# A two-layer graph network: where the edge lists of the nodes are built, and when the list writes are issued

## The chip, the cores and the metric

The kernel runs on one core of a Trainium2 chip. The core has five engines with instruction queues of their own: PE (TensorE: matmuls), DVE (VectorE), ACT (ScalarE), POOL (GpSimd) and SP (SyncE, which here only issues transfers). The metric is the device time of one launch in microseconds (us); lower is better. Each engine executes its instructions in the order in which they were laid down, and waits at one of them until what it needs is there. Indirect transfers (gather: rows of a table by a list of indices; scatter: rows to a table by a list of indices) are issued by POOL, plain transfers by SP or ACT.

## What is computed

There are 1250 nodes with 768 features and 20000 directed edges, sorted by destination, with one of 34 types each.

```
h  = relu(layernorm(x))
h  = gatv2(h, 8 heads, W1s, W1d, attn1) ; h = layernorm(h + relu(layernorm(x)))
h  = gatv2(h, 1 head, Wos, Wod, attno)  ; x = x + layernorm(h)
gatv2: fs = x Ws + bs ; fd = x Wd + bd ; per edge e = leaky_relu(fs[src] + fd[dst]) . attn
       softmax of e over the edges of a destination ; out = elu(sum alpha * fs[src])
h  = relu(layernorm(x))
mean[r, n] = mean of h[src] over the edges of type r into node n
h1 = sum over r of mean[r] W_rel[r] + h W_root + b
out = x + gcn(h1)        (symmetric normalisation by degrees + 1, one dense layer)
```

## The kernel before

Nodes are handled in ten tiles of 128, ordered by falling degree, so that a tile needs as many edge slots as its first node has edges: `CAPS = (33, 22, 20, 18, 17, 16, 15, 14, 13, 11)`, 179 slots in all. One slot of one tile is called a row here: for each of 128 nodes, one source node.

**Front** (`fast_front`). It loads x and edges, normalises x (`norm_scale`, L782 to L788) and transposes it (`to_columns`). Four things follow.

- The table: `sources(j)` (L807) makes tile j of `f_fs_d`, the projected sources with eight extra columns, by 26 matmuls on PE, two copies on ACT and a store on SP. `head_sums` (L795) makes the extra columns of the weights on DVE. Its PSUM tiles share the tag "ag" (two buffers, in the order written) with the ranking's.
- The ranking: L752 to L772 count for each node how many rows of 32 edges end before it, ten gathers (L777, `got`) fetch the row in which its edges begin, and `first` (L829) is the number of its first edge; the degree is the difference of neighbours, for which one matmul (L832) fetches the next partition's value. Keys of degree and number are spread to all partitions by matmuls (L859, L860) and compared by ten instructions (L865); the sum is the rank. Ten scatters (L880) write number, first edge and degree by rank into `rank_d`, and L901 reads it back in ranked order.
- The edges, after the ranking and in ranked order: ten gathers (L912) fetch 64 packed edges per node from `win_d`, and L916 to L931 shift them to the node's first edge, into `f.ell` and the source numbers `f.srci`.
- `pairs()` (L937 to L1069): for each edge the place in a list by type, with two sets of matmuls (L970 to L979) that count over partitions, and much DVE work. Its result goes to DRAM (`place_d`, L1069).

What sets the order: the program is laid down engine by engine by a planner with a cost model of its own. Of the instructions that it holds ready for an engine it takes the one written first; `tc.issue_after(i)` adds that an instruction comes behind `i` on its engine. In the front the table's tiles 0 and 1 are put around L832, keys behind tile 1, and tile 2 behind keys, by hand.

**Attention 1** (`attention`, called at L1444). For each row one gather (L1148) fetches 128 source rows into one of 24 buffers (`ring`), and three DVE instructions make z (L1208, L1213) and its sums (L1214). Rows are taken in chunks of at most 20; after a chunk comes its softmax, then ACT scales the rows and PE adds them (L1258 to L1268). After a tile's last chunk `finish1` (L1420) normalises, makes the rows of the second layer's tables and scatters them (`fs2`, by `scatter` at L1152). `negated1` fetches a tile's own rows (`h`) and makes the destination term `nfd` with 24 matmuls on PE.

**The lists.** Beside attention 1, 179 scatters (L1152, `r_pair_d`), one for each row, write the edges' records into `pair_d` by their places. They have no work of their own before them but `pairs()`, and a fill: `prepare_lists` (L1349) writes padding records into all of `pair_d` and zeros behind two later tables, makes these in SBUF and loads the places back (L1375). `list_edges(row, n)` (L1385) adds `n` to a count and issues as many writes behind the gather `row`. It is called with 0.9 after each row but the first 20, and with 60 after the very last, which issues all that are left (36).

Attention 2 and the 34 types follow, and a last dense layer. They are not touched.

Of the kernel before, what the change touches and what calls it, by code (L numbers as in the profile page):

```python
# [18 lines left out]
P = 128  # L19
# [607 lines left out]
def fast_front(ctx, tc, f, x, src, dst, edge_type, W1s, b1s, W1d, b1d, attn1, attno, W_rel):  # L627
# [34 lines left out]
    rank_d = dram.tile([NP, 4], I32, name="f_rank_d")  # L662
# [9 lines left out]
    f.ell = keepp.tile([P, NT, S0], I32, name="f_ell")  # L672
# [4 lines left out]
    f.place_d = dram.tile([P, NT * S0], I32, name="f_place_d")  # L677
    f.w1d = const.tile([P, KC, D], F32, name="f_w1d")

    with ExitStack() as front:  # L680
# [110 lines left out]

        quarter = SLOPE / (1.0 - SLOPE)
# [29 lines left out]
        last = sources(0)  # L822
# [8 lines left out]
        with tc.issue_after(last.ins):  # L831
            last = nc.tensor.matmul(sh_ps[:, 0:1], shift, first[:, 0:1], start=True, stop=True)  # L832
        with tc.issue_after(last.ins):
            last = sources(1)
# [3 lines left out]


# [14 lines left out]
        with tc.issue_after(last.ins):  # L854
            for g in range(2):
                wide = ps_m.tile([P, 2, 512], F32, name="wide", tag="ag").rearrange("p a b -> p (a b)")
                for lo, hi in ((0, 512), (512, N // 2)):
                    at = slice(g * (N // 2) + lo, g * (N // 2) + hi)
                    nc.tensor.matmul(wide[:, lo:hi], ones16[:EP], flat2[:, at], start=True, stop=False)  # L859
                    last = nc.tensor.matmul(wide[:, lo:hi], big16[:EP], flat[:, at], start=False, stop=True)  # L860
                nc.scalar.copy(keys[:, g * (N // 2):(g + 1) * (N // 2)], wide[:, :N // 2])
# [7 lines left out]
        rec = prep.tile([P, NT, 4], I32, name="rec")  # L869
        nc.vector.memset(rec, 0)  # L870
        nc.vector.tensor_copy(rec[:, :, 0], node)
        nc.vector.tensor_copy(rec[:, :, 1], first[:, :NT])
        nc.vector.tensor_copy(rec[:, :, 2], deg)

        past = prep.tile([NP - N, 4], I32, name="past")
# [10 lines left out]
        with tc.issue_after(last_keys.ins):  # L886
            sources(2)


        packed = prep.tile([EP, EC], I32, name="packed")  # L890
        nc.vector.scalar_tensor_tensor(packed, ev[:, 2, :], 2048.0, ev[:, 0, :], op0=ALU.mult, op1=ALU.add)
        zrow = prep.tile([1, RW], I32, name="zrow")
        nc.vector.memset(zrow, 0)
        pk = packed.rearrange("p (r c) -> p r c", c=RW)
        nc.scalar.dma_start(win_d[1:NR + 1, :RW].rearrange("(p r) c -> p r c", p=EP), pk)
        nc.scalar.dma_start(win_d[0:NR, RW:].rearrange("(p r) c -> p r c", p=EP), pk)
        nc.scalar.dma_start(win_d[NR:NR + 1, RW:], zrow)


        rk = prep.tile([P, NT, 4], I32, name="rk")  # L900
# [3 lines left out]
        nc.vector.tensor_copy(f.degf, rk[:, :, 2])  # L904
        arow = prep.tile([P, NT], I32, name="arow")
        nc.vector.tensor_scalar(arow, rk[:, :, 1], 5, None, op0=ALU.arith_shift_right)
        nc.vector.tensor_scalar(arow, arow, float(NR - 1), 1.0, op0=ALU.min, op1=ALU.add)
        offs = prep.tile([P, NT], I32, name="offs")
        nc.vector.tensor_scalar(offs, rk[:, :, 1], RW - 1, None, op0=ALU.bitwise_and)
        win = prep.tile([P, NT, WIN], I32, name="win")  # L910
        for k in range(NT):
            nc.gpsimd.indirect_dma_start(  # L912
                out=win[:, k, :], out_offset=None, in_=win_d[:, :],
                in_offset=bass.IndirectOffsetOnAxis(ap=arow[:, k:k + 1], axis=0))
        wf = prep.tile([P, NT, WIN], F32, name="wf")
        nc.vector.tensor_copy(wf, win)  # L916
        bits = prep.tile([P, 5, NT], F32, name="bits")
        for i in range(5):
            bi = prep.tile([P, NT], I32, name="bi", tag="bi", bufs=2)
            nc.vector.tensor_scalar(bi, offs, i, 1, op0=ALU.arith_shift_right, op1=ALU.bitwise_and)  # L920
            nc.vector.tensor_copy(bits[:, i, :], bi)
        for i in (4, 3, 2, 1, 0):
            b = 1 << i
            L = S0 + b - 1
            df = prep.tile([P, NT, S0 + 15], F32, name="df", tag="df")
            nc.vector.tensor_sub(df[:, :, :L], wf[:, :, b:b + L], wf[:, :, :L])
            nc.vector.tensor_tensor(df[:, :, :L], df[:, :, :L],
                                    bits[:, i, :, None].to_broadcast([P, NT, L]), op=ALU.mult)
            nc.vector.tensor_add(wf[:, :, :L], wf[:, :, :L], df[:, :, :L])
        nc.vector.tensor_copy(f.ell, wf[:, :, :S0])  # L930
        nc.vector.tensor_scalar(f.srci, f.ell, 2047, None, op0=ALU.bitwise_and)  # L931
# [5 lines left out]
        def pairs():  # L937
# [13 lines left out]
            typ = pp.tile([P, NT, S0], I32, name="typ")  # L951
            nc.vector.tensor_scalar(typ, f.ell, 11, None, op0=ALU.arith_shift_right)
            tv = pp.tile([P, NT, S0], F16, name="tv")
            nc.vector.scalar_tensor_tensor(tv, pad, 100.0, typ, op0=ALU.mult, op1=ALU.add)
# [101 lines left out]
            pl_i = pp.tile([P, NT, S0], I32, name="pl_i")  # L1056
# [11 lines left out]
            nc.vector.scalar_tensor_tensor(pl_i, pad, float(P * COLS), pl, op0=ALU.mult, op1=ALU.add)  # L1068
            nc.sync.dma_start(f.place_d[:, :], pl_i.rearrange("p k s -> p (k s)"))  # L1069

        for j in range(3, NT):
            sources(j)
# [53 lines left out]
def fast_rest(ctx, tc, f, x, src, dst, edge_type, W1s, b1s, W1d, b1d, attn1, ln1_w, ln1_b,  # L1126
# [9 lines left out]
    h2_d = dram.tile([NP + P, D], F32, name="r_h2_d")  # L1136
    ZERO = NP + (PT + 1) * P
    h1_d = dram.tile([ZERO + 1, D], F32, name="r_h1_d")
    pair_d = dram.tile([P * f.COLS, 3], I32, name="r_pair_d")
# [11 lines left out]
    def scatter(table, rows, idx, group, **kw):  # L1151
        s = nc.gpsimd.indirect_dma_start(  # L1152
            out=table, out_offset=bass.IndirectOffsetOnAxis(ap=idx, axis=0), in_=rows, in_offset=None, **kw)
        tc.declare_no_dep(s.ins, group=group, reason="every node's row is written once")
        tc.add_to_no_dep_group(group, s.ins)

# [15 lines left out]
    def attention(H, table, negated, attn_e, first, loads, finish, rate, rest):  # L1172
# [21 lines left out]
        def front(c, i):  # L1194
# [5 lines left out]
            if s >= CHUNK or t.k:  # L1200
                list_edges(row, rate)
            if t.k == NT - 1 and s == t.S - 1:
                list_edges(row, rest)
            if t.lg is None:
# [144 lines left out]
    def prepare_lists():  # L1349
# [3 lines left out]
        with tc.tile_pool(name="r_fill", bufs=1, side="right") as fp:  # L1353
            lane = rp.tile([P, 1], F32, name="lane")
            nc.gpsimd.iota(lane, pattern=[[0, 1]], base=NP, channel_multiplier=1,
                           allow_small_or_imprecise_dtypes=True)
            fill = fp.tile([P, COLS, 3], I32, name="fill")
            nc.vector.memset(fill[:, :, 2], 0)
            ones_c = fp.tile([P, COLS], F32, name="ones_c")
            nc.vector.memset(ones_c, 1.0)  # L1360
# [10 lines left out]
            for t in range(PT + 1):  # L1371
                nc.sync.dma_start(h1_d[NP + t * P:NP + (t + 1) * P, :], zero)
# [362 lines left out]
```

## Time and profile before

| | us |
|---|---|
| median of nine runs | 2773.75 |
| lowest and highest | 2768.9, 2782.42 |
| the profiled execution | 2778.29 |
| its span in the profile | 2776.4 |
| busy: PE, DVE, POOL, ACT | 2359.7, 1566.6, 1525.5, 854.1 |
| first row gathered, first z | 153.9, 184.3 |
| first and last list write | 221.4, 853.6 |
| first gather of attention 2 | 899.7 |

Times in the profile count from the start of the span. "Busy" is the sum of an engine's instructions; issuing, waiting and branching are not in it. In the timeline a line gives the start, the duration, the engine, the line of the program and the operation, output<-inputs, and in brackets how long the engine was idle before it and who ended that. A window's line gives, after its length, the busy time of PE, of PE's weight loads, of DVE, ACT and POOL with their instructions in brackets, then the granted PE clock, the busy share of the DMA engines and GB/s.

### The profile page before, as it was taken

How to read it: one execution, taken by the hardware profiler on the slowest of the kernel's cores; microseconds unless marked ns; L12 is line 12 of the kernel's file. 1: busy time of each engine (PE TensorE's matmuls, PEld its weight loads, DVE VectorE, ACT ScalarE, POOL GpSimd, SP SyncE). 2: the span in 40 equal slices, each digit the busy share in tenths (PEclk: the TensorE clock that was granted, in tenths of full speed). 3: DMA queues.
4: the chain of work that ended last, by engine and by line, in shares of the span. 5: the costliest groups of instructions: out<-in, count | busy, mean ns of one | idle time of the engine just before them, and what ended most of it. 6: DMA issues, size and time to landing. Idle time of an engine off the chain costs nothing. (4 is left out here: it accounts for less than half of the span.)

```text
span 2776.4 us, 24188 instructions
## 1 busy us (share of the span) xinstructions
PE 2359.7 (85%) x7759; PEld 1369.0 (49%) x7759; DVE 1566.6 (56%) x2361; ACT 854.1 (31%) x2308; POOL 1525.5 (55%) x1113
## 2 busy tenths in 40 slices
PE   6953685788888386888789999999999999999688
PEld 3521242444444143544456666666666666666254
DVE  5599979998975999999363222222222322210262
ACT  3004765767762132333311211221212211212010
POOL 1343877777873776776275554444444554431471
PEclk9976897999989788999889999999999999999899
DMA  6155443444431866675387777777777777766783
GB/s 212 44 165 181 128 131 97 128 132 134 137 93 38 278 203 202 208 216 178 123 265 189 191 190 192 185 189 197 192 193 199 187 188 189 182 162 152 213 266 121
DMA packets 136548, 476.85 MB, mean 172 GB/s; under 512 B 26185, under 2 KB 28514, under 8 KB 136413
## 3 DMA queue, kind: packets, MB, share of 16 engines
q0 software_dynamic: 83712, 334.44, 46.6%
q1 hardware_dynamic: 48043, 134.21, 13.6%
q10 hardware_dynamic: 4658, 6.57, 0.7%
q8 instruction: 64, 1.05, 0.2%
q14 instruction: 71, 0.58, 0.1%
HBM read 385.91 MB, written 89.33 MB: 171 GB/s over the span
## 5 line engine op out<-in xcount | busy, mean ns | idle before, releaser
L1116 PE MATMUL ps<-wrel,mT 128*128 128x384 f32 x3336 | 1099.6, 486 | 1.0 <-DMA wrel<-in_L_gnn_W_rel_dram 1.0
L1116 PEld LDWEIGHTS ps<-wrel,mT 128*128 128x128 f32 x3336 | 623.4, 190 | 407.2 <-issue 1.3
L1148 POOL DMA_INDIRECT g<-r_h_d,lists x241 | 340.4, 1413 | 525.6 <-DVE g L1580 286.2
L1268 PE MATMUL ag<-fs,identf 128*128 128x384 f32 x716 | 290.7, 540 | 165.4 <-ACT fs L1266 155.7
L1580 DVE TENSOR_TENSOR g<-g,g 128x768 f32<-128x768 f32 x68 | 64.6, 949 | 614.7 <-DMA g<-r_h_d,lists 420.5
L1208 DVE TENSOR_TENSOR z<-fs,nfd 128x776 f32<-128x776 f32 (+1 forms) x358 | 348.1, 990 | 45.2 <-DMA fs<-f_fs_d,rec 24.5
L1266 ACT ACTIVATE fs<-fs,lg 128x96 f32<-128x96 f32 x1376 | 370.7, 364 | 2.2 <-issue 1.7
L1258 PE MATMUL ag<-fs,dg 128*128 128x384 f32 x716 | 249.2, 509 | 81.1 <-ACT dg L1256 42.8
L1148 POOL DMA_INDIRECT fs<-f_fs_d,rec x179 | 251.1, 1403 | 101.1 <-issue 47.6
L1268 PEld LDWEIGHTS ag<-fs,identf 128*128 128x128 f32 x716 | 135.8, 205 | 307.6 <-ACT fs L1266 237.8
L1603 POOL DMA_INDIRECT r_h_d<-y,lists x139 | 224.1, 1612 | 109.8 <-ACT y L1602 52.1
L1148 POOL DMA_INDIRECT fs<-r_fs_d,rec x179 | 238.9, 1334 | 81.8 <-issue 31.4
L1152 POOL DMA_INDIRECT r_pair_d<-rec,place x179 | 234.8, 1311 | 85.1 <-issue 47.3
L1258 PEld LDWEIGHTS ag<-fs,dg 128*128 128x128 f32 x716 | 140.6, 199 | 186.1 <-ACT dg L1256 88.0
L1602 ACT ACTIVATE y<-ps,lists 128x768 f32<-128x768 f32 x71 | 64.1, 902 | 479.5 <-PE ps L1116 479.5
L1602 ACT ACTIVATE y<-ps,rcnt 128x768 f32<-128x768 f32 x68 | 61.4, 902 | 455.3 <-PE ps L1116 455.3
L1210 DVE SCALAR_TENSOR_TENSOR z<-z,attn_o 128x769 f32<-128x769 f32 x179 | 176.9, 1007 | 0.6 <-ACT dg L1256 0.5
L1665 DVE TENSOR_TENSOR acc<-acc,nb 128x768 f32<-128x768 f32 x69 | 66.2, 959 | 187.1 <-DMA nb<-r_h_d,srcz 183.3
L1213 DVE TENSOR_TENSOR z<-z,attn 128x776 f32<-128x776 f32 x179 | 168.6, 957 | 0.1
L1214 DVE TENSOR_REDUCE lg<-z 128x8 f32<-128x776 f32 x179 | 168.3, 952 | 0.1
L1513 DVE SCALAR_TENSOR_TENSOR arow<-node,from_f,arow 128x1250 f16<-128x1250 f16 x110 | 166.2, 1511 | 1.7
L1106 ACT COPY mT<-pt 128x384 f32<-128x384 f32 x278 | 119.2, 486 | 26.1 <-PE pt L1104 26.1
(283 smaller groups left out, 2298.6 us busy)
## 6 DMA issues: line engine op xcount, KB each, us to landing
wrel<-in_L_gnn_W_rel_dram SPq DMA_DIRECT2D x37, 2304.0 KB
g<-r_h_d,lists POOLq DMA_INDIRECT x241
r_nfd_d<-fd SPq DMA_DIRECT2D x10, 384.0 KB
nfd<-r_nfd_d SPq DMA_DIRECT2D x10, 384.0 KB
r_x_d<-xb SPq DMA_DIRECT2D x10, 384.0 KB
x1r<-r_x_d SPq DMA_DIRECT2D x10, 384.0 KB
f_fs_d<-o_s SPq DMA_DIRECT2D x9, 388.0 KB
x<-in_x_dram SPq DMA_DIRECT2D x9, 384.0 KB
```

What stands on the lines that cost most here:

```text
L1116: last = nc.tensor.matmul(ps[:n, half, :f.HW], hT[:, k, j * P:j * P + n], w[:, k, cols], start=(k == 0), stop=(k == f.KC - 1 and not bias))
L1148: return nc.gpsimd.indirect_dma_start(out=to, out_offset=None, in_=table, in_offset=bass.IndirectOffsetOnAxis(ap=idx, axis=0))
L1152: s = nc.gpsimd.indirect_dma_start(out=table, out_offset=bass.IndirectOffsetOnAxis(ap=idx, axis=0), in_=rows, in_offset=None, **kw)
L1208: nc.vector.tensor_tensor(z, fs, t.nfd, op=ALU.max)
L1210: nc.vector.scalar_tensor_tensor(z[:, 0, :], z[:, 0, :], 1.0, attn_e[:, 0, :], op0=ALU.mult, op1=ALU.mult, accum_out=t.lg[:, s, :])
L1213: nc.vector.tensor_mul(z, z, attn_e)
L1214: nc.vector.tensor_reduce(t.lg[:, s, :], z, axis=AX.X, op=ALU.add)
L1258: nc.tensor.matmul(c.ps[:, half, :HW], dg, fs[:, 0, half * HW:(half + 1) * HW], start=begin, stop=end)
L1266: nc.scalar.activation(fs[:, h, :HD], fs[:, h, :HD], AF.Copy, scale=t.lg[:, s, h:h + 1])
L1268: nc.tensor.matmul(c.ps[:, half, :HW].rearrange("p (h d) -> p h d", d=HD), f.identf, fs[:, half * H // 2:(half + 1) * H // 2, :HD], start= ...
L1513: nc.vector.scalar_tensor_tensor(a, node16, from_f[:, k, s:s + 1], a, op0=ALU.is_equal, op1=ALU.add)
L1603: s = nc.gpsimd.indirect_dma_start(out=h1_d[:, :], out_offset=bass.IndirectOffsetOnAxis(ap=j.node, axis=0), in_=y, in_offset=None, compute ...
```

## The change

1. **Edges in node order.** The edges are fetched and shifted for the nodes in their own order, from `first`, not from the ranked order. `arow`, `offs` and the ten gathers now stand right behind `first`, the shift behind the compares. The ranked record grows from 4 numbers to 2 + 33: number, degree and the 33 edges. Behind the read-back two instructions split source and type (`f.typ`); `f.ell` is gone.
2. **Order on PE.** L832 and the keys come without table tiles before them; tile 0 is behind the keys' last matmul, and tiles 1 to 9 are written after it.
3. **The fill in the front.** The padding records, the zeros and their eight stores are made behind the transposes of x, in the front's own pool.
4. **Places stay in SBUF.** `f.place` is written by DVE; the way over `place_d` is gone.
5. **List writes.** 30 behind row 23 of tile 0 (the last that has a free buffer), 0.85 behind each later row, 4 behind the last row, 7 behind the `fs2` scatter of tile 7, and what is left (7) behind that of tile 8.

```diff
-    rank_d = dram.tile([NP, 4], I32, name="f_rank_d")
+    rank_d = dram.tile([NP, 2 + S0], I32, name="f_rank_d")
...
-    f.place_d = dram.tile([P, NT * S0], I32, name="f_place_d")
+    f.place = keepp.tile([P, NT, S0], I32, name="place")
...
+        lane = keepp.tile([P, 1], F32, name="lane")
+        nc.gpsimd.iota(lane, pattern=[[0, 1]], base=NP, channel_multiplier=1,
+                       allow_small_or_imprecise_dtypes=True)
+        fill = prep.tile([P, COLS, 3], I32, name="fill")
...
+        nc.sync.dma_start(f.pair_d.rearrange("(p c) f -> p c f", p=P), fill)
+        zero = prep.tile([P, D], F32, name="zero")
+        nc.vector.memset(zero, 0.0)
+        nc.sync.dma_start(f.h2_d[NP:, :], zero)
+        for t in range(PT + 1):
+            nc.sync.dma_start(f.h1_d[NP + t * P:NP + (t + 1) * P, :], zero)
+        nc.sync.dma_start(f.h1_d[f.ZERO:, :], zero[:1])
...
-        last = sources(0)
...
-        with tc.issue_after(last.ins):
-            last = nc.tensor.matmul(sh_ps[:, 0:1], shift, first[:, 0:1], start=True, stop=True)
-        with tc.issue_after(last.ins):
-            last = sources(1)
+        nc.tensor.matmul(sh_ps[:, 0:1], shift, first[:, 0:1], start=True, stop=True)
...
+        arow = prep.tile([P, NT], I32, name="arow")
+        begin = prep.tile([P, NT], I32, name="begin")
+        nc.vector.tensor_copy(begin, first[:, :NT])
+        nc.vector.tensor_scalar(arow, begin, 5, None, op0=ALU.arith_shift_right)
+        nc.vector.tensor_scalar(arow, arow, float(NR - 1), 1.0, op0=ALU.min, op1=ALU.add)
...
+        for j in range(NT):
+            nc.gpsimd.indirect_dma_start(
+                out=win[:EP, j, :], out_offset=None, in_=win_d[:, :],
+                in_offset=bass.IndirectOffsetOnAxis(ap=arow[:EP, j:j + 1], axis=0))
...
-        with tc.issue_after(last.ins):
-            for g in range(2):
+        for g in range(2):
...
-        nc.vector.tensor_copy(rec[:, :, 1], first[:, :NT])
-        nc.vector.tensor_copy(rec[:, :, 2], deg)
+        nc.vector.tensor_copy(rec[:, :, 1], deg)
+        nc.vector.tensor_copy(rec[:EP, :, 2:], wf[:EP, :, :S0])
...
         with tc.issue_after(last_keys.ins):
-            sources(2)
+            sources(0)
...
-        nc.vector.tensor_copy(f.ell, wf[:, :, :S0])
-        nc.vector.tensor_scalar(f.srci, f.ell, 2047, None, op0=ALU.bitwise_and)
+        nc.vector.tensor_scalar(f.srci, rk[:, :, 2:], 2047, None, op0=ALU.bitwise_and)
+        nc.vector.tensor_scalar(f.typ, rk[:, :, 2:], 11, None, op0=ALU.arith_shift_right)
...
-            nc.vector.scalar_tensor_tensor(pl_i, pad, float(P * COLS), pl, op0=ALU.mult, op1=ALU.add)
-            nc.sync.dma_start(f.place_d[:, :], pl_i.rearrange("p k s -> p (k s)"))
-
-        for j in range(3, NT):
+            nc.vector.scalar_tensor_tensor(f.place, pad, float(P * COLS), pl, op0=ALU.mult, op1=ALU.add)
+
+        for j in range(1, NT):
             sources(j)
...
-            if s >= CHUNK or t.k:
+            if t.k == 0 and s == ring - 1:
+                list_edges(row, 30)
+            elif t.k or s >= ring:
                 list_edges(row, rate)
...
-        f.place = rp.tile([P, NT, S0], I32, name="place")
-        nc.sync.dma_start(f.place, f.place_d.rearrange("p (k s) -> p k s", k=NT))
...
-            scatter(fs2_d[:, :], fs, f.perm[:, k:k + 1], "fs2")
+            row = scatter(fs2_d[:, :], fs, f.perm[:, k:k + 1], "fs2")
+            if NT - 4 < k < NT - 1:
+                list_edges(row, 7 if k < NT - 2 else 40)
...
-        attention(H, f.fs_d, negated1, f.attn_1, prepare_lists, loads1, finish1, 0.9, 60)
+        attention(H, f.fs_d, negated1, f.attn_1, prepare_lists, loads1, finish1, 0.85, 4)
```

The code of the fill in `prepare_lists`, of the packed edges and of the shift (L889 to L931) is removed at its old place and stands unchanged at the new one.

## Prediction, made before the result was known

> **What bounds the kernel now.** The one profiled execution took 2778.3 us (span 2776.4 and 1.9 around it), 4.5 over the median of nine, 2773.75; sums below are on its span. I read the stages first (busy time per window), because all edits lie before 855 us.
>
> ```profile
> 100.00:150.00 50.00, 49.31 (x157) 24.36 (x156) 33.45 (x90) 5.96 (x15) 9.85 (x11) 1.00 0.17 57
> 150.00:200.00 50.00, 21.96 (x90) 13.31 (x90) 48.23 (x101) 3.29 (x9) 30.04 (x27) 0.69 0.68 220
> 200.00:250.00 50.00, 6.06 (x17) 3.12 (x16) 49.83 (x74) 4.96 (x15) 3.34 (x3) 0.58 0.54 196
> 250.00:300.00 50.00, 33.10 (x71) 12.50 (x70) 47.59 (x65) 37.60 (x143) 40.91 (x27) 0.84 0.41 111
> ```
>
> After the window's length come PE, its weight loads, DVE, ACT and POOL. PE is full to 150 us, DVE from 150 to 250, while POOL is nearly idle from 200 to 250. From 250 on POOL shows 40.91 busy, but each of its 27 instructions is also preceded by 0.3 us: it is full too. Then the timeline, engine by engine:
>
> ```profile
> 57.04 0.38 PE L832 MATMUL sh_ps<-first,shift 128*128 128x1 f32 x2
> 67.17 0.39 PE L859 MATMUL wide<-diag,ones 125*128 125x512 f16 x1
> 147.09 0.89 PE L814 MATMUL ps<-bias,ones_row 1*98 1x388 f32 x2
> 147.91 0.32 PE L970 MATMUL pp<-mask,tri 128*128 128x340 bf16 x1
> ```
>
> PE has the ten table tiles (L813) from 35.8 to 148.0, with the ranking's matmuls between them, and the pairs' matmuls (L970) directly behind the last one. The degrees wait for PE until 57, the ranking until 67.
>
> ```profile
> 50.77 0.15 DVE L829 SCALAR_TENSOR_TENSOR first<-before,within 128x10 f32<-128x10 f32 x1
> 129.24 0.29 DVE L939 TENSOR_SCALAR tri<-iota_f,iota_p 128x128 bf16<-128x128 f32 x1
> 163.02 0.18 DVE L1002 TENSOR_SCALAR more<-tot 128x34 f32<-128x34 f32 x1
> 212.82 0.49 DVE L1068 SCALAR_TENSOR_TENSOR pl_i<-pad,pl 128x330 int32<-128x330 f32 x1
> ```
>
> The pairs begin at 129.2 on DVE. The first 33.5 us of them need nothing from PE's pairs' matmuls; from L1002 on they do. Places are done at 213.3.
>
> ```profile
> 152.67 0.94 POOL L1148 DMA_INDIRECT h<-f_h_d,f_permg  x1 [35.34 <-ACT tot L981]
> 221.43 1.37 POOL L1152 DMA_INDIRECT r_pair_d<-rec,place  x1 [30.80 <-DMA r_pair_d<-fill]
> 251.06 3.36 POOL L1148 DMA_INDIRECT fs<-f_fs_d,rec  x1 [25.68 <-PE ag L1268]
> 427.65 2.29 POOL L1148 DMA_INDIRECT fs<-f_fs_d,rec  x1 [0.30 <-DMA fs<-f_fs_d,rec]
> 430.24 2.35 POOL L1152 DMA_INDIRECT r_pair_d<-rec,place  x1 [0.30 <-issue]
> 853.57 0.97 POOL L1152 DMA_INDIRECT r_pair_d<-rec,place  x1 [0.30 <-issue]
> ```
>
> POOL fetches 24 rows to 188, then idles 30.8 us for the fill and 25.7 us for a free row buffer. Where each row's fetch ends 2.9 to 5 us before the z that reads it, POOL is the bound: rows 24 to 48 (254 to 335 us) and again 469 to 676. Between, and after 676, rows lie ready 8 to 38 us: DVE, ACT and PE bound there. The last 36 list writes run from 801 to 854, while the last z is at 835.6 and the next fetch at 899.7.
>
> **Part 1, the ranking ahead of the table (front).** `first` comes at 50.9. I add 1 us (bounds 0 and 9.6): the fill's 2.7 MB are now written near 20 us, and DMA ran at 283 GB/s to 50 us, so they are 9.6 us of traffic that the small `got` gathers share. With PE free, L832 starts at 52 instead of 57.0. From there to the key matmuls took 2.6 us besides PE's wait (57.04 to 59.6); 0.5 is added for the four new small DVE rows, so keys start at 55 instead of 67.2. Rank compares: 2.5 later, 10 x 1.56, to 73.1. The edges' fetch (10 x 1.25) fits beside them. Decoding (119.1 to 128.5, and 1.2 of bits) now follows the compares: 84.3. Ten rank scatters and reading back took 18.5 (85.7 to 104.2): 103. So pairs start near 104, 25 us earlier, and need 33.5: they would reach L1002 at 137.5.
>
> But the table is now last on PE. Tiles took 9.9 each (8 tiles in 79.2). Ten from 56.6 are 99; 2 more because PE starts cold (12 matmuls took 6.09 after the idle time at 46, 4.18 later): the end is 157.6, 9.6 after 148.0 (bounds +6.6 and +18). The pairs' matmuls come behind it in program order, so 20 of the 25 us end as DVE idle time. `tot` came 2.1 after them, the third 6.6: L1002 runs at 159.8 (before 163.0), the rows needing the third at 164.2 (before 166.3). From there on the same work: places at 211.2, first z at 182.2, both **2.1 us earlier**. POOL's first row fetch is 9.6 later, near 163.5, and its 24 rows (34.2 us) and two h rows end by 201: still before the places.
>
> **Part 2, the fill.** Its DVE rows (216.0 to 218.5, 2.6 with the zero row) go under the wait for inputs at 1.5 to 7 us, where DVE idles 3.0 and 1.95; if that cover is gone they would delay `first` by up to 2.6, which the upper bound above holds. Its 8 DMAs on SP move ahead of the h0 stores, needed only at 152. With the places kept in SBUF, POOL no longer waits 8.1 us (213.3 to 221.4) for two transfers and the fill. Row 23's z (260.5) moves by 2.1 + 2.6 to 255.8.
>
> **Part 3, 30 writes behind row 23.** They fill POOL's idle time from 211.3. Their price beside DVE is unknown: the burst of 36 took 1.49 each (801.1 to 854.9, issue in), the three at 221 to 225 1.4; in 425 to 440 POOL got one instruction per 2.62 us. I take 1.49, the same kind of instruction in a row: row 24's fetch starts at 211.3 + 44.7 = 256, before 251.1. That is 5 later, but before, rows 24 to 26 took 5.2 each beside a full DVE, to 264.9. Now DVE runs out of rows at 255.8, and rows go at 2.7 (266.5 to 282.8, six rows): row 26 ends at 257.0 + 5.4 = 262.4. **-2.5.** At 2.62 to 243, 1.49 to 255.8 and 1.29 after (the pitch at 369 to 385, DVE idle): 12 + 8.6 + 9.4 writes, row 24 at 267.9, row 26 about **+9.5**.
>
> [...]
>
> **Part 4, 0.85 for 0.9.** Rows 24 to 48: 25 x 0.05 writes x 1.64 (POOL's pitch there) = **-2**. 469 to 676: 57 x 0.05 x 1.78 (207 us for 116 instructions) = 5.1 at most, 0 if the ring of row buffers holds POOL back instead (it idled 7 us there at 619); I take **-3**.
>
> **Part 5, the tail.** 36 writes become 4, 7 and the last 7 between table rows. The burst ended 45 us before the next fetch and only table row 7's write stood behind it (ready at 834.6, its buffer reused at 869.5): 0. Uncovered, 14 writes would be 21 us.
>
> Sum: -2.5 - 2 - 3 = -7.5 (the -2.1 and -2.6 are inside the first, as when DVE runs dry). 2778.3 - 7.5 = 2770.8; less 4.5, a median near 2766.
>
> **Rivals.** (a) The list writes starve, and POOL is late at row 24: +9.5 - 5 = +4.5, and if the rest go at 1.49 instead of 1.29, +6.4: 2778 to 2780, slower. For it: the locked stretch at 425; against: 36 writes without one over 1.65 us. It decides from 1.74 us a write on (0.25 x 30 = 7.5). (b) Pairs' matmuls come between table tiles: places near 172, row 24 at 201 + 45 = 246, 10 earlier: 2756. Against: L970 stood behind every table tile. (c) Fill traffic delays `first` by the whole 9.6: about 8 back, 2774. For it: the saturated DMA; against: small fetches share engines, `got` landed 1.8 us after its last issue. (d) POOL is not what rows wait for after 335: -3 is nothing and part of -2.5, 2771.
>
> **How the numbers follow.** Forecast 0.38, (a) 0.28, (b) 0.10, (c) 0.12, (d) 0.12. 0.2% is 5.5 us, about what a measurement can tell. Faster by more: 0.26 of the forecast, (b) 0.10, some of (c) and (d) 0.05: 0.41. Slower: 0.21 of (a), 0.06 of (c): 0.27 (a planned order that shifts elsewhere is in there). The rest, 0.32, within. Range: (b) with a little more below, (a) and 5 us of changed order above: 2752 to 2784; the forecast alone 2760 to 2773.
>
> **What would show it.** Right: keys near 55, pairs from 104, a DVE gap of about 20 us before L1002's row, the last table tile near 157, 30 writes from 211 to 256, row 24 fetched near 256, and from there the same stages 5 to 8 us earlier. Wrong: pairs' matmuls before the last table tile; writes over 1.74 us apart; table tiles starting later than 60 us; or engine orders after 335 that differ from before, since the planner lays them out anew.

## The result and the profile after

The changed kernel takes 2798.4 us (median of 10 runs, 2792.85 to 2800.94), the kernel before on the same chips 2774.42 (31 runs). The ratio is 1.008, with a 95% interval of 1.0067 to 1.0093: **slower by 0.8%**, some 22 us, outside the predicted range. The profiled execution has a span of 2789.2 us. Profiles of one kernel differ by several us from execution to execution (the changed kernel's two have spans of 2789.2 and 2799.1 us); so the stages below are read from the profiles, and what a change is worth from the ratios.

The windows of the changed kernel, in the order of columns used before (length; busy time of PE, its weight loads, DVE, ACT, POOL; granted PE clock, DMA share, GB/s):

```profile
100.00:150.00 50.00, 39.51 (x106) 20.10 (x107) 34.76 (x88) 4.45 (x11) 3.73 (x4) 0.86 0.14 45
150.00:200.00 50.00, 39.75 (x155) 21.03 (x153) 23.35 (x56) 5.48 (x14) 18.42 (x16) 0.86 0.42 135
200.00:250.00 50.00, 11.39 (x30) 6.54 (x30) 50.00 (x64) 2.24 (x3) 38.49 (x21) 0.61 0.73 236
250.00:300.00 50.00, 28.48 (x57) 10.42 (x58) 30.83 (x40) 34.54 (x125) 40.91 (x30) 0.77 0.16 38
```

Before, PE was busy for 49.31 of the fifty us behind 100 (now 39.51), and DVE was full from 150 to 250. Now DVE has 23.35 of 50 between 150 and 200, and a second hole, 30.83 of 50, behind 250. Each hole has its own cause. The first, in the timelines of PE, of ACT and of DVE:

```profile
98.49 0.91 PE L840 MATMUL ps<-bias,ones_row 1*128 1x388 f32 x2
110.49 5.94 PE L839 MATMUL ps<-w1s,hT 128*128 128x388 f32 x10 [11.09 <-ACT o_s L844]
```

```profile
80.33 0.18 ACT L844 COPY o_s<-ps 128x8 f32<-128x8 f32 x1
109.38 0.30 ACT L1374 ACTIVATE dinv<-f_degf,f_ones_col 128x10 f32<-128x10 f32 x1 [28.87 <-DVE f_degf L952]
109.59 0.78 ACT L843 COPY o_s<-ps 128x768 f32<-128x768 f32 x1
110.33 0.81 ACT L843 COPY o_s<-ps 128x768 f32<-128x768 f32 x1
```

```profile
174.47 0.18 DVE L1023 TENSOR_SCALAR more<-tot 128x34 f32<-128x34 f32 x1 [29.83 <-ACT tot L1002]
```

One small ACT instruction, the square root of the degrees (`dinv`, L1374), was laid down between the copies of table tiles 1 and 2. It waits 28.9 us for the ranked degrees. The copies of tiles 2 and 3 stand behind it, both PSUM buffers of the table stay full, and PE stops for 11.1 us. The table ends at 172.3 instead of 157.6 as predicted, and `more` waits 29.8 us for it. The places come at 226.3 (before: 213.3), the first z at 197.3 (184.3), row 23's z at 270.9 (260.5).

The second hole, in POOL's and DVE's timelines:

```profile
226.53 2.37 POOL L1168 DMA_INDIRECT r_pair_d<-rec,place  x1 [5.55 <-DVE place L1088]
229.21 2.29 POOL L1168 DMA_INDIRECT r_pair_d<-rec,place  x1 [0.30 <-issue]
231.80 2.29 POOL L1168 DMA_INDIRECT r_pair_d<-rec,place  x1 [0.30 <-issue]
...
260.90 3.96 POOL L1168 DMA_INDIRECT r_pair_d<-rec,place  x1 [0.30 <-issue]
...
285.76 0.97 POOL L1168 DMA_INDIRECT r_pair_d<-rec,place  x1 [0.30 <-issue]
287.04 0.99 POOL L1164 DMA_INDIRECT fs<-f_fs_d,rec  x1 [0.30 <-issue]
```

```profile
228.80 0.95 DVE L1233 TENSOR_TENSOR z<-z,attn 128x776 f32<-128x776 f32 x1
229.68 0.95 DVE L1228 TENSOR_TENSOR z<-fs,nfd 128x776 f32<-128x776 f32 x1
230.55 0.95 DVE L1234 TENSOR_REDUCE lg<-z 128x8 f32<-128x776 f32 x1
...
270.92 0.95 DVE L1228 TENSOR_TENSOR z<-fs,nfd 128x776 f32<-128x776 f32 x1
291.04 0.97 DVE L1228 TENSOR_TENSOR z<-fs,nfd 128x776 f32<-128x776 f32 x1 [19.17 <-DMA fs<-f_fs_d,rec]
```

A write issued at 229.21 ends at 231.50, 0.95 behind the start of the next TENSOR_REDUCE (230.55): it is held while DVE multiplies and takes the maximum. So the first ten writes come 2.59 to 2.67 us apart, one cycle of DVE. Behind them DVE has a softmax between the rows and then takes two rows at a time, and the spacing lies between 1.27 and 4.26. The 30 writes take 60.5 us, 2.02 each on average, against 1.49 in the prediction; row 24's gather comes at 287.0, and DVE, out of rows since 271.9, is idle for 19.2 us. Row 24's z is 29.7 later than before: 10.4 from the front, 19.3 from this hole.

### The profile page after: what moved, and what is told of

Its sections match the earlier page's. It is cut to its first block, busy times and chain, and to the rows that moved or that the text cites. A ratio compares the mean times of both kernels' runs of the same rounds, so it can differ in the third digit from the quotient of the medians.

```text
span 2789.2 us, 24175 instructions
## 1 busy us (share of the span) xinstructions
PE 2362.5 (85%) x7759; PEld 1368.8 (49%) x7759; DVE 1565.1 (56%) x2360; ACT 855.2 (31%) x2308; POOL 1535.9 (55%) x1113
## 5 line engine op out<-in xcount | busy, mean ns | idle before, releaser
L1164 POOL DMA_INDIRECT fs<-f_fs_d,rec x179 | 242.5, 1355 | 82.1 <-issue 47.8
L1602 POOL DMA_INDIRECT r_h_d<-y,lists x139 | 223.3, 1606 | 108.5 <-ACT y L1601 50.8
L1168 POOL DMA_INDIRECT r_pair_d<-rec,place x179 | 249.6, 1395 | 59.9 <-issue 48.6
```

What stands on the lines that cost most here:

```text
L1164: return nc.gpsimd.indirect_dma_start(out=to, out_offset=None, in_=table, in_offset=bass.IndirectOffsetOnAxis(ap=idx, axis=0))
L1168: s = nc.gpsimd.indirect_dma_start(out=table, out_offset=bass.IndirectOffsetOnAxis(ap=idx, axis=0), in_=rows, in_offset=None, **kw)
L1602: s = nc.gpsimd.indirect_dma_start(out=h1_d[:, :], out_offset=bass.IndirectOffsetOnAxis(ap=j.node, axis=0), in_=y, in_offset=None, compute ...
```

## The experiments

The ratios below are against the kernel before on the same chip, with 95% intervals.

### The two halves of the change apart

`front_only` is the changed kernel with the old list schedule; `lists_only` is the kernel before with the new one.

```diff
 front_only, against the changed kernel
-            if t.k == 0 and s == ring - 1:
-                list_edges(row, 30)
-            elif t.k or s >= ring:
+            if s >= CHUNK or t.k:
                 list_edges(row, rate)
...
-            row = scatter(fs2_d[:, :], fs, f.perm[:, k:k + 1], "fs2")
-            if NT - 4 < k < NT - 1:
-                list_edges(row, 7 if k < NT - 2 else 40)
+            scatter(fs2_d[:, :], fs, f.perm[:, k:k + 1], "fs2")
...
-        attention(H, f.fs_d, negated1, f.attn_1, prepare_lists, loads1, finish1, 0.85, 4)
+        attention(H, f.fs_d, negated1, f.attn_1, prepare_lists, loads1, finish1, 0.9, 60)
```

`lists_only` makes the same edit the other way round in the kernel before.

> The changed kernel with the list writes scheduled as before (0.9 behind each row but the first 20, all that are left behind the last row). Theory 1 (two terms: the new front brings row data later, and the 30 writes keep row 24's gather back): the places come near 226 and each z of the first rows about 10.5 us later than before, as in the changed kernel; row 24's gather then waits for a free row buffer as before, near 261, and DVE doesn't run dry; 10 us of the 24 stay, a median near 2784. Theory 2 (the 30 writes alone cost the time, the later front is absorbed by waits behind it): within 3 of 2774. Theory 3 (the front alone): near 2798.

> The kernel before with only the new list schedule (30 behind row 23, 0.85, 4, 7 and the rest); ranking, table order, fill and place transfer stay as before. Theory 1: the writes begin at 221 and take 2.62 us each beside a full DVE until DVE runs out of rows near 260, 1.27 after that; row 24's gather is issued near 221 + 15 x 2.62 + 15 x 1.27 = 280, 29 later than before, DVE is idle for about 20 us in front of it; 3 come back by the rate of 0.85 and up to 10 in the last tile: median 2781 to 2791. Theory 2: near 2798. Theory 3: 2774.

Measured: `front_only` **1.0057** (1.0037 to 1.0076), `lists_only` **1.0017** (1.0004 to 1.0030). In `front_only` the places come at 225.9, row 23's z at 270.6, and row 24's gather waits for a row buffer as before, at 261.2; its z is 10.1 later than before. So the front alone costs as much as theory 1 said, or more (0.57% is 16 us, against 10 expected). In `lists_only` row 24's gather comes at 270.2, not at 280, since the writes are closer there: 47.8 us for 30. POOL's timeline of `lists_only`:

```profile
222.46 1.60 POOL L1152 DMA_INDIRECT r_pair_d<-rec,place  x1 [30.58 <-DMA r_pair_d<-fill]
224.37 0.99 POOL L1152 DMA_INDIRECT r_pair_d<-rec,place  x1 [0.30 <-issue]
225.67 0.97 POOL L1152 DMA_INDIRECT r_pair_d<-rec,place  x1 [0.30 <-issue]
...
228.22 1.03 POOL L1152 DMA_INDIRECT r_pair_d<-rec,place  x1 [0.30 <-issue]
...
270.21 1.00 POOL L1148 DMA_INDIRECT fs<-f_fs_d,rec  x1 [0.30 <-PE ag L1272]
```

Theory 2 (the writes alone) falls by both ratios. Theory 3 (the front alone) isn't excluded by the times: the 1.0057 of `front_only`, up to 1.0076, stands beside 1.0080, and 1.0067 when measured again, for the changed kernel, on other chips. Against it speaks that the hole in front of row 24 is there with the 30 writes only, and the next section, where the 30 writes cost time with the front repaired.

### The ACT instruction

```diff
+            f.last_copy = nc.scalar.copy(ov[:n, :, :, HD], ps[:n, :, HW:QW])
-            nc.scalar.copy(ov[:n, :, :, HD], ps[:n, :, HW:QW])
...
-        nc.scalar.activation(f.dinv, f.degf, AF.Sqrt, bias=f.ones_col, scale=1.0)
+        with tc.issue_after(f.last_copy.ins):
+            nc.scalar.activation(f.dinv, f.degf, AF.Sqrt, bias=f.ones_col, scale=1.0)
```

`sqrt_late` has this edit alone; `front_sqrt` has it with the old list schedule.

> The changed kernel with one ACT instruction moved: the square root of the degrees (dinv) is queued behind the last copy of the table instead of between the copies of tiles 1 and 2. Theory 1 (that instruction waits for the ranked degrees until 109, both PSUM buffers of the table fill up, and PE stands still from 99.4 to 110.5): no such stop; the table ends near 161 instead of 172.3, the places are done near 215 instead of 226, first z near 186; the median falls by about 10, to 2788. Rival (PE's stop is the slower clock or a missing record, or the rows wait for something else): the table's end moves by less than 3, median within 3 of 2798.

> The changed kernel with the square root behind the table's last copy and the list writes scheduled as before. Theory (the prediction's front terms hold once PE isn't stopped for 11 us): table's end near 161, places near 212, first z near 183, row 23's z near 256, row 24's gather near 247; 3 to 5 faster than before, 10 to 14 faster than the run with the new front and the old list schedule. Rival (the new front costs time in some other place too, for that run was 13 above before while its rows came only 10 later): 5 or more slower than before.

In `sqrt_late` PE goes through without a stop. PE's and ACT's timelines:

```profile
97.64 0.91 PE L840 MATMUL ps<-bias,ones_row 1*128 1x388 f32 x2
98.48 4.18 PE L839 MATMUL ps<-w1s,hT 128*128 128x388 f32 x12
```

```profile
157.95 0.80 ACT L843 COPY o_s<-ps 98x768 f32<-98x768 f32 x1 [8.93 <-issue]
...
158.71 0.32 ACT L1375 ACTIVATE dinv<-f_degf,f_ones_col 128x10 f32<-128x10 f32 x1
```

The table ends at 157.9, the places are done at 211.8, the first z is at 182.9 and row 23's at 256.5. The prediction had 157.6, 211.2, 182.2 and 255.8: its front was right but for this one instruction. Ratio **1.0055** (1.0032 to 1.0078), by the point values 0.25% less than the changed kernel, though on another chip, and 0.12% less than the changed kernel when measured again; so the expected fall by 10 us isn't shown by this run. The median (2779.03 beside 2765.35) stands 9 above its own profiled execution, and what happens in the executions without a profile isn't seen. `front_sqrt` settles it: **0.9992** (0.9981 to 1.0002), against 1.0057 (1.0037 to 1.0076) with the old place of the square root. The two ran on different chips, each beside the kernel before; the intervals are far apart. So this instruction alone costs 0.65% with the old list schedule, by the point values. The expected gain of 3 to 5 us against before isn't shown; 2 is the point value. The rival (a cost in some other place of the front) falls.

### The number of writes behind row 23, and the place of tile 0

`sqrt_12` takes 12 writes instead of 30, a rate of 0.8, and 24 writes behind table row 7's scatter; `tile0_12` also writes tile 0 of the table ahead of the ranking again.

```diff
-                list_edges(row, 30)
+                list_edges(row, 12)
...
-                list_edges(row, 7 if k < NT - 2 else 40)
+                list_edges(row, 24 if k < NT - 2 else 60)
...
-        attention(H, f.fs_d, negated1, f.attn_1, prepare_lists, loads1, finish1, 0.85, 4)
+        attention(H, f.fs_d, negated1, f.attn_1, prepare_lists, loads1, finish1, 0.8, 4)
...
 tile0_12 also
+        sources(0)
         gotf = prep.tile([P, NT, RW], F32, name="gotf")
...
         with tc.issue_after(last_keys.ins):
-            sources(0)
+            sources(1)
...
-        for j in range(1, NT):
+        for j in range(2, NT):
             sources(j)
```

> The changed kernel with the square root moved and the list schedule 12 behind row 23, 0.8 a row, 4, 24 and the rest. Theory (of the list part only the number behind row 23 cost time): the 12 writes end near 243, before a row buffer is free; row 24's gather near 248 instead of 273 with 30 writes; median 5 to 15 below the run with 30 writes, at or just below that of the kernel before. Rival (the rate and the tail matter as much): no better than the run with 30 writes.

> The same, and the table's tile 0 again before the ranking's matmuls, as in the kernel before. Theory (the table's end sets when pairs go on and when rows can be fetched): the table ends near 152, 10 earlier; places near 203, first z near 175, row 23's z near 248; 7 to 11 faster than before. Rival (rows are held by the ring's buffers and DVE): within 3 of the run without this edit.

> The fastest version so far (square root moved, tile 0 ahead of the ranking, list schedule 12, 0.8, 4, 24, rest) once more, beside the two others. Theory: again 7 to 11 faster than the kernel before; writes 2.62 apart, 12 of them in 35 us, as DVE leaves the places in SBUF here. Rival (the first measurement was a lucky chip): under 5.

`sqrt_12`: **0.9989** (0.9980 to 0.9998), against 1.0055 with 30 writes; row 24's gather comes at 248.3 instead of 272.7. The two ran on different chips. Three more kernels with 30 writes and the square root moved, which come further below, have 1.0018, 1.0036 and 1.0041, so the 30 writes cost 0.3 to 0.7%. `tile0_12`: **0.9961** (0.9946 to 0.9975), and in a later session **0.9924** (0.9892 to 0.9956): 11 and 21 us by the point values, **faster than the kernel before** and the fastest version here. Row 23's z is at 250.7. POOL's timeline of the second one shows why 12 writes are free and 30 are not:

```profile
206.53 2.37 POOL L1169 DMA_INDIRECT r_pair_d<-rec,place  x1 [5.54 <-DVE place L1089]
209.21 2.29 POOL L1169 DMA_INDIRECT r_pair_d<-rec,place  x1 [0.30 <-issue]
...
234.70 1.74 POOL L1169 DMA_INDIRECT r_pair_d<-rec,place  x1 [0.30 <-issue]
241.54 3.35 POOL L1165 DMA_INDIRECT fs<-f_fs_d,rec  x1 [5.10 <-PE ag L1289]
```

They end 5.1 us before a row buffer is free. By the 2.62 us of a write, one more would still fit, and from the second on each would delay row 24; that was not tried.

### The fill, with the old front

`fill_early` moves the fill into the front of the kernel before and keeps the places in SBUF; `old_front_lists` adds the list schedule of `sqrt_12`. The edits are those lines of the change, without the ranking's.

> The kernel before with only the fill made in the front and the places kept in SBUF. By the prediction's part 2: DVE's 2.6 us between 216 and 218.5 go, nothing else on the path moves, since row 24's gather still waits for a free row buffer: median near 2771.5. Rival (the fill's 2.7 MB delay the rows of edges that the ranking fetches: `first` came at 53.3 in the changed kernel and at 50.8 before): `first` near 53, the places no earlier, median 2774 to 2777.

> The kernel before with the fill in the front, the places in SBUF and the list schedule 12, 0.8, 4, 24, rest; ranking and table as before. Theory: the 12 writes run from 216 to 248, while POOL waits for a row buffer; row 24's gather stays at 251; the lower rate gives 4 us on rows 24 to 48 and up to 10 from 469 to 676: 8 to 14 faster than before. Rival: the row buffers or DVE hold these rows, gain under 3.

`fill_early`: **0.9999** (0.9987 to 1.0012). Row 23's z is at 260.6, not 2.6 earlier: `first` came at 53.2, against 50.8 and 50.4 in two profiles of before. But in kernels without the early fill it came at 52.3 and 56.1 too, so whether the fill's traffic delays it isn't settled. The fill's DVE rows did leave the place where they were: from the first z to row 23's z the profile has 73.6 us instead of 76.1, about the 2.6 of the prediction. But not all of them went under the wait for inputs: six, 1.1 us together, run at 33.1, where DVE works for the front. `old_front_lists`: **0.9990** (0.9977 to 1.0003); the lower rate and the other tail give 2.8 us by the point value, which is the rival's number, and 6 at the end of the interval. The expected 8 to 14 are excluded.

### Pairs' matmuls between table tiles

`between` calls `pairs()` behind table tile 7, with `dinv` moved; `between_lists` adds the schedule with 12 writes.

```diff
-        for j in range(1, NT):
-            sources(j)
+        for j in range(1, 8):
+            last = sources(j)
+        pairing = ExitStack()
+        pp = pairing.enter_context(tc.tile_pool(name="f_pp", bufs=1, side="right"))
+        with tc.issue_after(last.ins):
+            pairs()
+        for j in range(8, NT):
+            sources(j)
```

> The changed kernel with the pairs' matmuls written between table tiles 7 and 8 and the square root behind the table's last copy; list schedule unchanged (30 behind row 23). Theory (DVE's 29.8 us wait in front of `more` is for PE's table, and the 30 writes are then what is late): no such wait, places near 197 instead of 226, row 23's z near 241, writes from 197 to 257, row 24 near 257 against 251 before and 287 after; median within 6 of the kernel before. Rival (the rows' fetch, 10 us behind the table's end, becomes the bound, or buffers are freed later): row 23's z after 255, median like that of the sqrt run.

> The same with 12 writes behind row 23, 0.8 behind later rows, 4 behind the last row, 24 behind table row 7's scatter and the rest behind table row 8's. Theory: 12 writes at 2.62 fit into the time in which POOL waits for a row buffer anyway; row 24's gather near 235, its z near 243 (before: 251 and 261); 0.1 writes fewer per row give 4 us on rows 24 to 48 and up to 10 on 469 to 676; the tail stays hidden: 20 to 30 us faster than before. Rival (what follows, ACT's scaling and the dense layer of a finished tile, sets the pace): gain under 10.

Both expectations were wrong (within 6 us of the kernel before, and 20 to 30 us faster): **1.0100** (1.0081 to 1.0119) and **1.0053** (1.0038 to 1.0068). `more` comes at 145.0 and the places at 179.8, 46 earlier than in the changed kernel, but the first z only at 201.8. POOL's timeline of `between`:

```profile
180.65 0.99 POOL L1170 DMA_INDIRECT h<-f_h_d,f_permg  x1 [73.99 <-DVE nfd L1212]
181.94 0.97 POOL L1170 DMA_INDIRECT fs<-f_fs_d,rec  x1 [0.31 <-issue]
...
218.24 3.69 POOL L1170 DMA_INDIRECT fs<-f_fs_d,rec  x1 [0.30 <-issue]
222.24 1.02 POOL L1174 DMA_INDIRECT r_pair_d<-rec,place  x1 [0.30 <-issue]
```

The table ended at 164.6, and yet the first gathers start at 180.6, 0.9 behind the end of `pairs()`. In this version the tiles of `pairs()` were opened while the ranking's were still held, and probably lie where attention's buffers come; that was not tried. The 24 gathers follow, and the writes, queued behind row 23, start at 222; row 23's z is at 294.7. Places 46 us earlier were worth nothing here, as the rows weren't there.

### What holds a write

`one_input` leaves out part of the computation: for the rows of tile 0, z is the maximum of the row and zero, times 0.5, so that both instructions have one SBUF input.

```diff
-            nc.vector.tensor_tensor(z, fs, t.nfd, op=ALU.max)
+            nc.vector.tensor_scalar(z, fs, 0.0, None, op0=ALU.max)
...
-                nc.vector.tensor_mul(z, z, attn_e)
+                nc.vector.tensor_scalar(z, z, 0.5, None, op0=ALU.mult)
```

> The changed kernel, and for the rows of tile 0 both two-input DVE instructions of z are replaced by one-input ones (maximum with zero instead of with the destination term, times 0.5 instead of times the attention vector), so part of the computation is left out there. Theory (a write waits while DVE runs an instruction with two SBUF inputs, and goes through while it runs one with one input): beside the full DVE behind the places the 30 writes are 1.27 to 1.5 us apart, and row 24's gather comes some 40 us behind the first write instead of 60. Rival (any busy DVE, or the writes' own transfers, hold POOL): writes still 2 to 2.6 us apart while DVE is busy.

The timelines of POOL and DVE:

```profile
235.56 2.75 POOL L1168 DMA_INDIRECT r_pair_d<-rec,place  x1 [0.31 <-issue]
```

```profile
235.50 1.02 DVE L1229 TENSOR_SCALAR z<-fs 128x776 f32<-128x776 f32 x2
236.45 1.02 DVE L1237 TENSOR_SCALAR z<-z 128x776 f32<-128x776 f32 x2
237.39 1.81 DVE L1240 TENSOR_REDUCE lg<-z 128x8 f32<-128x776 f32 x2
```

The theory as I had put it falls: the write, 2.75 us long, is held through four one-input instructions of 0.55 us too (those with two inputs take 0.95), and ends 0.92 behind the start of TENSOR_REDUCE. The 30 writes take 47.2 us, neither the 40 of the theory nor 2 to 2.6 each: a row is shorter on DVE now (1.81 us where rows go singly), the writes there come one to a row, and DVE runs out of rows at 256.

`lists_only` speaks against it as well: there the three DVE instructions of the changed kernel let two writes through in each cycle:

```profile
227.46 0.95 DVE L1217 TENSOR_TENSOR z<-z,attn 128x776 f32<-128x776 f32 x1
228.22 1.03 POOL L1152 DMA_INDIRECT r_pair_d<-rec,place  x1 [0.30 <-issue]
228.33 0.95 DVE L1212 TENSOR_TENSOR z<-fs,nfd 128x776 f32<-128x776 f32 x1
229.21 0.95 DVE L1218 TENSOR_REDUCE lg<-z 128x8 f32<-128x776 f32 x1
```

The write that starts near the end of the multiplication passes beside the maximum (`z<-fs,nfd`) in 1.03 us, though that has two SBUF inputs too. The first write of this kernel (222.46, 1.60 us) starts 0.25 into a multiplication and ends 0.98 behind the start of the maximum, about as long as a free write takes (0.97): here the multiplication holds a write, and the maximum doesn't. In the changed kernel both do, and a write takes 2.29 to 2.37 us. So two SBUF inputs alone don't decide it. Five more runs bear on that.

```diff
 phase, with the square root moved
+                nudge = rp.tile([P, 8], I32, name="nudge")
+                with tc.issue_after(row.ins):
+                    row = nc.gpsimd.tensor_copy(nudge, f.place[:, 0, :8])
                 list_edges(row, 30)
...
 late_place, with the square root moved
-    f.place = keepp.tile([P, NT, S0], I32, name="place")
...
+        f.place = rp.tile([P, NT, S0], I32, name="place")
         f.pairs()
...
 via_dram: places stored to place_d and loaded back, as before
```

> The changed kernel with the square root moved and one small POOL instruction (a copy of eight places) between row 23's gather and the 30 writes, so that the first write starts at another point of DVE's cycle of three instructions. Theory (what decides between 1.31 and 2.62 us a write is the point of DVE's cycle at which the first write starts; a start within the sum over a row, TENSOR_REDUCE, lets two writes through in each cycle): writes 1.28 to 1.35 apart while DVE computes rows, row 24's gather about 48 us behind the first write instead of 60.6, near 260; median 5 to 10 below the run without this instruction. Rival (places that DVE has written, or this order on DVE, always cost 2.62): 60 us, row 24 near 273, no difference in time.

> The changed kernel once more. Theory of the fixed point of start: the same spacing, 2.6 us for the first ten writes, 60 us in all; table's end near 172; ratio near 1.008. Rival (the spacing is chance): another spacing in this execution.

> The kernel before with the new list schedule once more. If the point of start follows DVE, 1.28 to 1.35 us a write again and 48 us in all; since here a transfer releases the first write, it may also fall into 2.62, and then row 24's gather comes near 281.

> The changed kernel with the square root moved, and the places stored to DRAM and loaded back as in the kernel before (the tile then also lies at the old address). Theory A (how the places come into SBUF, or where they lie, decides): writes 1.28 to 1.35 apart while DVE computes rows, some 48 us in all; the first write about 5 us later for the two transfers, row 24's gather near 265 instead of 272.7. Theory B (the new front's order on DVE decides): 2.62 and 60 us, row 24 near 278.

> The changed kernel with the square root moved, and the places written by DVE into a tile that lies where it lay in the kernel before (2 KB further on). If the address decides: writes 1.28 to 1.35 apart, 48 us in all, row 24's gather near 260, median 5 to 10 below the run with the square root alone. If it is that DVE has written them, or that DVE releases the first write: 2.62 and 60 us.

| run | ratio (95%) | 30 writes, us | one write beside full DVE |
|---|---|---|---|
| the changed kernel again | 1.0067 (1.0043 to 1.0090) | 60.6 | 2.6 |
| `lists_only` again | 1.0011 (0.9989 to 1.0034) | 47.7 | 1.28 and 1.34 in turn |
| `phase` | 1.0018 (0.9999 to 1.0038) | 59.0 | 1.35 once, then 2.62 |
| `via_dram` | 1.0041 (1.0025 to 1.0057) | 57.4 | 2.6 |
| `late_place` | 1.0036 (1.0021 to 1.0051) | 60.5 | 2.6 |

The changed kernel and `lists_only` keep their spacing in a second execution. It isn't the point of DVE's cycle at which a write starts: in `phase` the second write starts 0.78 us into a multiplication and is held for 1.93, where `lists_only` has 1.03 from 0.76 on. It is not who brings the places into SBUF (`via_dram`) and not where they lie (`late_place`, `via_dram`). It isn't the order of the new front either, for `old_front_lists` has 2.62. What the two kernels with 1.3 (the kernel before, in its three writes at 221, and `lists_only`) have in common is that the fill is still made by DVE shortly before the writes (217.3 to 219.7 in `lists_only`); in all the others it is made in the front. That was not tried apart, and moving the fill also moves other tiles. Nor is it fixed for a whole kernel: the kernel before has 2.62, too, from 412 to 438, and in the changed kernel a write at 532.01, which starts 0.80 into a multiplication, passes the maximum in 1.03 us. **The cause stays open.**

### The kernel before, profiled again

> The kernel before, unchanged, on the chip of these runs, for its profile. If its last tile took longer only in the first profile: from the first z of tile 9 to its last 33 to 34 us as in all other runs, instead of 43.9, and the first gather of attention 2 near 886 instead of 899.7. If it belongs to the kernel: 43 to 44.

In the first profile of before, tile 9's rows took 43.9 us, here 32.6: that belonged to one execution. The first gather of attention 2 is at 893.0, not at 886; in the two profiles of the changed kernel it is at 913.3 and 916.4, 20 and 23 later, like the medians.

## Why the prediction was wrong

- **Part 1, the table on PE** ("ten from 56.6 are 99; 2 more because PE starts cold: the end is 157.6"). This step failed. PE started at 58.7 and kept 9.9 us a tile, but stood still for 11.1 us, and the first ten of the twelve matmuls afterwards took 5.9 us (all twelve 6.6) where twelve take 4.2. The sum looked at PE, DVE and POOL, and put the wait for ACT, whose copies empty the table's PSUM buffers, at nothing. The instruction could be seen in ACT's timeline of the kernel before:

```profile
104.53 0.30 ACT L1377 ACTIVATE dinv<-f_degf,f_ones_col 128x10 f32<-128x10 f32 x1 [14.92 <-DVE f_degf L904]
104.74 0.78 ACT L817 COPY o_s<-ps 128x768 f32<-128x768 f32 x1
```

  There it waited 14.9 us, and the copy behind it was 6 us late, which the second PSUM buffer covered. In the change the degrees are known at 109.2 instead of 104.3, the copy behind the instruction is due at 89.5 instead of 98.6, so it is 20 us late, of which one tile of 9.9 is covered. Price: 0.65% with the old list schedule.
- **Part 1, the rest.** With that instruction moved, the table's end, the places, the first z and row 23's z came within 0.7 us of the predicted numbers in `sqrt_late`. Part of that is luck: PE began the table at 57.9, 1.3 later than in the sum, and its first twelve matmuls took 5.1, so 0.9 more than 4.2 where the sum had added 2. In the six profiled kernels with this front the table ends at 157.9 to 159.7 and row 23's z is at 256.5 to 259.5, up to 3.7 above the sum. In the changed kernel pairs began at 110.8 instead of 104, because DVE waited 6.6 us for the edges and the rank writes then waited for the shifted edges (ready at 89.8). With the table last on PE this shortened the wait in front of `more` and cost nothing.
- **Part 2, the fill** (-2.6): the gain on DVE between the first z and row 23's z came (73.6 us for 76.1), but alone it gave no time (0.9999), as `first` was later in that execution and row 24 waited for a row buffer as before.
- **Part 3, 30 writes at 1.49** (-2.5): the price of a write was mis-sized. It came from a burst at the end, beside a DVE with gaps and other instructions; beside a full DVE it is 2.62, and 2.02 over the 30, past the 1.74 from which rival (a) was to decide. That the writes fill POOL's idle time and then push row 24 back was right. The dearer sum beside it, row 24 at 267.9, was nearer to the 272.7 of `sqrt_late`; but it has only 12 writes at 2.62, to 243, and takes 1.49 from there to 255.8. With all writes at 2.62 until DVE runs out it would be 17 writes to 255.8 and 13 at 1.29: 272.6. What the writes cost: 0.66% between 1.0055 with 30 and 0.9989 with 12, 0.3% by the cheapest of the other kernels with 30.
- **Parts 4 and 5** (-3, -2 and 0): not seen against the scatter. The lower rate and tail of `old_front_lists` and `sqrt_12` move the time by 0.1% or less, by the point values.
- **The rivals.** (a) happened. (b) was priced at 2756; `between` had earlier places and was slower, so its price was wrong as far as that kernel stands for it. (c) `first` came 2.5 later, far from 9.6. (d) was not tried by itself; the 2.8 us of `old_front_lists` fit it. That PE could stop was among none of them. With the PE stop mended the 30 writes leave 1.0018 to 1.0055, some 2779 to 2790 on these chips, about the upper end of the range; the stop alone, in `front_only`, gives 2790. Both together are clearly outside it.

How the two costs add up is only roughly known: 0.65% and 0.63% each alone over `front_sqrt`, 0.88% both together (0.75% when measured again), and the 0.63% is the dearest of four kernels. At row 24 the profiles show them added (10.4 and 19.3 us); how much is given back behind it isn't resolved by the scatter.

## What to carry to other kernels

When work is moved forward on one engine, follow also the engine that empties its buffers, and read what stands in that engine's queue: here an ACT instruction of 0.30 us that waited 28.9 us for its data held the copies behind it, and a second buffer hid a delay of 6 us, but not one of 20, with a tile of 9.9 us. Take the price of an instruction from rows beside the same neighbours, not from the nearest burst: here a write beside a full DVE cost 2.62 us where 1.49 was taken, and 12 fit where 30 did not. In these runs a gain that freed one engine earlier was worth only what the next resource (row buffers, the table's end) could take: in `fill_early` 2.6 us on DVE gave 0.9999, in `between` places 46 us earlier gave 1.0100.

## What was not expected of the hardware

A write that POOL issued beside DVE was held by one-input TENSOR_SCALARs of 0.55 us (`one_input`, a write of 2.75 us) as well as by two-input instructions of 0.95 us (the changed kernel, 2.29 us); the two ended 0.92 and 0.95 behind the start of a TENSOR_REDUCE. Beside the same DVE cycle of 2.62 us, some kernels get one write through (the changed kernel, 2.6 us a write) and some two (`lists_only`, 1.28 and 1.34), the same in both executions of these two. What differs is whether the maximum of two tiles holds a write or lets it pass (1.03 us); the cause was not found. After an idle time of 11.1 us PE ran its first ten matmuls in 5.94 us in the changed kernel (after 11.3 in 5.72 in its second profile), where twelve take 4.18.
